# Low scores placed directly in front of the context product, and VectorE's sums and transposes interleaved, in a cross-attention block

## The chip, the cores and the metric

The kernel runs on one core of one Trainium2 chip. The metric is the device time of one execution, in microseconds. Three executions of the kernel before took 1654.61, 1655.78 and 1656.57 us, with a median of 1655.78 us. One further execution was profiled; its own time was 1652.77 us, and the span from its first to its last instruction was 1651.0 us.

## The reference

The block is one transformer layer with cross attention: 128 sequences of 128 tokens, 256 features, 16 heads of 16, a hidden layer of 1024, all in float32. Query i may see only keys j < i, so query 0 sees none and its attention is set to zero.

```python
q = (query @ Wq + bq).reshape(b, s, 16, 16).transpose(0, 2, 1, 3)
k = (key @ Wk + bk)...            # the same for k and v
scores = jnp.einsum('bhqd,bhkd->bhqk', q, k) / jnp.sqrt(16)
scores = jnp.where(j < i, scores, -1e30)
attn = jax.nn.softmax(scores, axis=-1);  attn = attn.at[:, :, 0, :].set(0.0)
ctx = jnp.einsum('bhqk,bhkd->bhqd', attn, v)
x = layer_norm(query + ctx @ Wo + bo, ln1_g, ln1_b)
out = layer_norm(x + jax.nn.relu(x @ W1 + b1) @ W2 + b2, ln2_g, ln2_b)
```

## The kernel before

Two sequences make a pair, and there are 64 pairs. The loop at line 778 makes one **step** for each pair p from 2 to 63. A step is a software pipeline over several pairs: it computes the scores and the softmax of pair p, the context and the first norm of pair p-1, the projections of pair p+1, and the feed-forward layers of pairs p-2 (`hidden`) and p-3 (`second`). The order on TensorE (PE), VectorE (DVE), ScalarE (ACT) and GpSimd (POOL) is exactly the order of the calls in the loop, because a manual schedule is set for these four engines. Only SyncE (SP), which issues most of the transfers, is put in order by the scheduler.

The queries of a sequence are split in two halves of 64. The upper half (`hi` = 1) can see all 128 keys, the lower half (`hi` = 0) only the first 64, so the lower half has half the work. `scores(p, hi)` is a set of small matmuls, with weights of 32 rows by 64 columns. `mask` adds the mask on DVE out of PSUM, `maximum` finds the row maximum on DVE and subtracts it on POOL, `exponential` runs on ACT, and `sums` adds up the rows and takes reciprocals on DVE and multiplies on POOL. These parts work on 8 of 16 heads at a time for the upper half (`ONE`, `TWO`) and on all 16 for the lower half (`ALL`).

The weights of the softmax have to be transposed for the context product. `turn(p)` does this in two stages: three transposes of 32x32 blocks on DVE write the tile `tb`, and then 16 transfers issued by SP move the blocks across the partitions into the tile `pT` (line 409). `weigh(p)` is the context product, made of small matmuls with weights of 128 rows by 32 columns that read `pT`: for every m and s first the lower half (`vd`, line 443), then the upper half (`vz`, line 451). `context` copies its result on ACT, and `attention_out` multiplies by Wo. `attention_sum` adds the residual on DVE and takes the mean and variance (`stats`); POOL makes the deviation out of them (lines 490 and 491), and `norm1` applies it.

`hidden` and `second` are the two feed-forward products, with weights of 128x128. `feed(...)` takes them in half units: 16 matmul records each in the trace. In the steady state a step has `second(p-3, 0)`, `second(p-3, 1)` and both halves of `hidden(p-2)`. `finish` multiplies by the gain and adds the bias of the second norm on POOL, and `store` issues the output transfer on ACT's queue (line 547). `values_out` issues another transfer on ACT's queue (`vd<-vz`, line 313).

The first steps have a table of their own (`plan`, line 770), because there is not yet a feed-forward product to be done. There `turn_x1_on_pe` transposes the normed tokens on PE. Later `turn_x1` does it with one DVE transpose and five transfers (lines 244 and 247).

In the built program every transfer of SP and of ACT signals its landing on one of eight semaphores, which are taken in turn in the order of the program. A transfer waits at its issue until the transfer eight places ahead of it in that order has landed, whichever of the two engines issued it, unless an earlier wait of its engine covers this already.

The order of the calls within a steady step, up to the transposes, is:

```python
scores(p, 1); feed(first); scores(p, 0)
feed(then); weigh(p - 1); context(p - 1)
queries(p + 1); attention_out(p - 1); keys(p + 1); values(p + 1)
feed(finally_)          # both halves of hidden(p - 2)
```

Of the kernel before, what the change touches and what calls it, by code (L numbers as in the profile page):

```python
# [8 lines left out]
F32 = mybir.dt.float32  # L9
# [10 lines left out]
def tile_cross_attention_block(  # L20
# [56 lines left out]

    blocks_of, tokens_of = {}, {}

    def load(ps):  # L80

        n = len(ps)
        for which, src in (("x", x), ("c", c)):
# [303 lines left out]

    def turn(p):  # L390


        st = states[p]
        tb = soft.tile([P, NS, (H + HH) * 32], F32, tag="tb", name=f"tb_{p}")
        at = 0
        for hi in (1, 0):
            sm = st["sm", hi].rearrange("p h j -> p (h j)")
            for t in range(sm.shape[1] // 1024):
                nc.vector.transpose(  # L399
                    tb[:, :, at : at + 256].rearrange("p j (n a) -> p n j a", a=32),  # L400
                    sm[:, t * 1024 : (t + 1) * 1024].rearrange(
                        "p (n j a) -> p n j a", j=NS, a=32
                    ),
                )
                at += 256
        pT = soft.tile([P, NS, (H + HH) * 32], F32, tag="pT", name=f"pT_{p}")
        for i in range(NS):
            for j in range(NS):
                nc.sync.dma_start(  # L409
                    pT[32 * j : 32 * j + 32, i, :], tb[32 * i : 32 * i + 32, j, :]  # L410
                )
        st["pT"] = pT.rearrange("p i (n a) -> p i n a", a=32)
# [19 lines left out]
    def weigh(p):  # L432

        st = states[p]
        pT = st.pop("pT")
        pc = bank(f"pc_{p}")

        for m in range(KC):
            for s in range(2):
                at = (m * 2 + s) * P  # L440
                blocks = slice(2 * s, 2 * s + 2)
                for j in range(NS):
                    nc.tensor.matmul(  # L443
                        pc[32 * j : 32 * j + 32, at : at + HP],
                        st["vd"][:, s, 4 * m + j].rearrange("p e d -> p (e d)"),
                        pT[:, blocks, H + 2 * j + m, :],
                        start=True, stop=True,
                    )
                for e in range(2):
                    for j in range(NS):  # L450
                        nc.tensor.matmul(  # L451
                            pc[32 * j : 32 * j + 32, at + HP : at + P],
                            st["vz"][:, s, 4 * m + j, 2 * e : 2 * e + 2, :].rearrange(
                                "p e d -> p (e d)"
                            ),
                            pT[:, blocks, 4 * j + 2 * m + e, :],
                            start=(e == 0), stop=(e == 1),
                        )
        st["pc"] = pc
# [33 lines left out]
    def attention_sum(p):  # L493
        st = states[p]
        t1 = st["t1"] = ffn.tile([P, 2, D], F32, tag="t1", name=f"t1_{p}")
        nc.vector.tensor_tensor(
            t1, st.pop("po").rearrange("p (s d) -> p s d", s=2), st.pop("xb"), ALU.add
        )
        stats(p, t1, 1)
        deviation(p, 1)  # L500

    def norm1(p):
# [187 lines left out]
                    done.append(p)  # L690
        return done

    alone = (2, 3)

    def both(what, p):
        return [(what, p, 0), (what, p, 1)]
# [48 lines left out]
    attention_out(0)  # L745
    exponential(1, 1, TWO)
    attention_sum(0)
    queries(2)
    sums(1, 1, ONE)
    norm1(0)  # L750
# [7 lines left out]
    for which in "xc":  # L758
# [9 lines left out]


    plan = {  # L770
        2: ([("hidden", 0, 1)], both("second", 0), both("hidden", 1)),
        3: ([("second", 1, 0)], [("second", 1, 1)], [("hidden", 2, 0)]),
        4: ([("hidden", 2, 1)], [("second", 2, 0)], [("second", 2, 1)]),
        5: ([("hidden", 3, 0)], [("hidden", 3, 1)], [("second", 3, 0)]),
        6: ([("second", 3, 1)], [("hidden", 4, 0)], [("hidden", 4, 1)]),
    }
    waiting, late = [], []
    for p in range(2, NP):
        soon, end = p + 1 < NP, p == NP - 1
        first, then, finally_ = plan.get(  # L780
            p, ([("second", p - 3, 0)], [("second", p - 3, 1)], both("hidden", p - 2))
        )
        scores(p, 1)
        mask(p, 1, 0)
        maximum(p, 1, ONE)
        feed(first)
        mask(p, 1, 1)
        maximum(p, 1, TWO)
        scores(p, 0)
        mask(p, 0, 0)  # L790
        mask(p, 0, 1)
        exponential(p, 1, ONE)
        maximum(p, 0, ALL)
        exponential(p, 1, TWO)
        feed(then)
        sums(p, 1, ONE)
        sums(p, 1, TWO)
        summed = late + sum_up(first + then)
        exponential(p, 0, ALL)
        sums(p, 0, ALL)  # L800
        for q in waiting:
            finish(q)
        weigh(p - 1)
        context(p - 1)
        if soon:
            queries(p + 1)
        attention_out(p - 1)
        if not end:
            turn(p)
        attention_sum(p - 1)  # L810
        if soon:
            keys(p + 1)
        if p + 2 < NP:
            for which in "xc":
                tokens(p + 2, which)
        norm1(p - 1)
        if p > 5:
# [6 lines left out]
        if p <= 5:  # L824
            turn_x1_on_pe(p - 1)
        residual1(p - 1)
        for q in summed:
            stats(q, states[q]["t2"], 2)
        if soon:
            add_bo(p + 1)  # L830
        if p % 2 == 0 and p + 4 < NP:
            load([p + 4, p + 5])
            load_tokens(p // 2 + 2)
        for q in summed:
            scale_and_shift(q)
        feed(finally_[:1])
        if end:
            turn_on_pe(p, 1, range(4))
        feed(finally_[1:])
        late = sum_up(finally_)  # L840
        for q in summed:
            norm2(q)
        waiting = summed
# [9 lines left out]
    attention_out(p)  # L853
    second(p - 2, 1, range(FC // 2, FC))
    attention_sum(p)
    second_sum(p - 2)
    hidden(p - 1, range(FC))
    norm1(p)
# [76 lines left out]
```

## Time and profile before

| | busy in us, share of the span | instructions |
|---|---|---|
| PE, matmuls | 1615.4 (98%) | 16524 |
| PE, weight loads | 1342.8 (81%) | 16524 |
| DVE | 1312.6 (80%) | 1983 |
| POOL | 1275.4 (77%) | 1108 |
| ACT | 766.9 (46%) | 1505 |
| span 1651.0 us; profiled execution 1652.77 us; median 1655.78 us | | |

A matmul row in the trace is the time that one matmul is in the array; matmuls overlap, so the time that a block takes is read from the start of its first matmul to the start of what comes next. From the ninth step on, the first matmul of the upper scores comes every 24.77 to 24.82 us. Steps 2 to 8 took 30.95, 25.71, 26.67, 26.67, 21.35, 25.14 and 24.94 us by the same measure. The transfers of a step that matter here, with their median time from issue to landing in the page: 16 times `pT<-tb` 2.2 us, `out_dram<-t` 3.4 us, `vd<-vz` 2.7 us, `x1t<-tbx` 1.8 us, `x1T<-x1t` 3.3 us. Loads of x and of the context bring two pairs at a time, by 4 transfers each every second step.

### The profile page before, as it was taken

How to read it: one execution, taken by the hardware profiler on the slowest of the kernel's cores; microseconds unless marked ns; L12 is line 12 of the kernel's file. 1: busy time of each engine (PE TensorE's matmuls, PEld its weight loads, DVE VectorE, ACT ScalarE, POOL GpSimd, SP SyncE). 2: the span in 40 equal slices, each digit the busy share in tenths (PEclk: the TensorE clock that was granted, in tenths of full speed). 3: DMA queues.
4: the chain of work that ended last, by engine and by line, in shares of the span. 5: the costliest groups of instructions: out<-in, count | busy, mean ns of one | idle time of the engine just before them, and what ended most of it. 6: DMA issues, size and time to landing. Idle time of an engine off the chain costs nothing.

```text
span 1651.0 us, 41181 instructions
## 1 busy us (share of the span) xinstructions
PE 1615.4 (98%) x16524; PEld 1342.8 (81%) x16524; DVE 1312.6 (80%) x1983; ACT 766.9 (46%) x1505; POOL 1275.4 (77%) x1108
## 2 busy tenths in 40 slices
PE   7998999999999999999999999999999999999997
PEld 5777888888888888888888888888888888888876
DVE  4767888888888888888888888888888888888852
ACT  4544444444444444444444444444444444444442
POOL 4766878878878878878878878878878878878873
PEclk9999999999999999999999999999999999999999
DMA  8444456566556566655666556565656575556330
GB/s 162 88 104 100 104 138 136 127 151 133 129 128 135 130 148 134 125 133 135 129 146 135 127 130 136 130 146 128 134 134 133 130 149 128 126 134 133 92 87 19
DMA packets 478973, 208.28 MB, mean 126 GB/s; under 512 B 352064, under 2 KB 447296, under 8 KB 478784
## 3 DMA queue, kind: packets, MB, share of 16 engines
q1 hardware_dynamic: 394192, 180.72, 50.3%
q10 hardware_dynamic: 84592, 24.93, 6.2%
q8 instruction: 131, 2.15, 0.6%
q14 instruction: 58, 0.48, 0.1%
HBM read 69.22 MB, written 31.98 MB: 61 GB/s over the span
## 4 chain that ended last, share of the span: by engine, by line
PE 89%; DVE 5%; POOL 3%; issue 1%; DMA 1%; ACT 1%; SPq 1%; ACTq 0%; POOLq 0%; DVEq 0%
PE py L627 25%; PE ph L611 25%; PE pq L267 7%; PE pss L333 7%; PE pk L267 6%; PE pv L299 6%; PE po L470 6%; PE pc L451 3%; PE pc L443 3%; DVE sm L350 1%; DVE nmx L361 1%; POOL sm L383 1%; POOL sm L362 1%; PE py L639 1%; SPq L409 1%
## 5 line engine op out<-in xcount | busy, mean ns | idle before, releaser
L362 POOL TENSOR_TENSOR sm<-sm,nmx 128x1024 f32<-128x1024 f32 x192 | 364.3, 1898 | 219.4 <-DVE nmx L361 219.4
L611 PE MATMUL ph<-x1T,w 128*128 128x256 f32 x2048 | 454.5, 379 | 2.5 <-ACT x1T L601 2.5
L627 PE MATMUL py<-w,hT 128*128 128x256 f32 x1952 | 453.5, 385 | 0.0
L611 PEld LDWEIGHTS ph<-x1T,w 128*128 128x128 f32 x2048 | 388.3, 190 | 57.4 <-ACT x1T L601 3.5
L627 PEld LDWEIGHTS py<-w,hT 128*128 128x128 f32 x1952 | 361.0, 190 | 76.8 <-ACT hT L617 21.9
L350 DVE TENSOR_TENSOR sm<-pss,neg 128x1024 f32<-128x1024 f32 (+1 forms) x256 | 237.9, 950 | 212.6 <-PE pss L333 199.2
L369 ACT ACTIVATE sm<-sm 128x1024 f32<-128x1024 f32 x192 | 203.0, 1057 | 354.0 <-POOL sm L362 344.6
L383 POOL TENSOR_TENSOR sm<-sm,rs 128x1024 f32<-128x1024 f32 x192 | 359.2, 1898 | 2.6 <-DVE rs L382 2.4
L617 ACT ACTIVATE hT<-ph,b1e_c 128x256 f32<-128x256 f32 x512 | 214.1, 470 | 193.5 <-PE ph L611 159.6
L399 DVE STREAM_TRANSPOSE tb<-sm 128x1024 f32<-128x1024 f32 x183 | 220.4, 1231 | 32.2 <-POOL sm L383 22.3
L361 DVE TENSOR_REDUCE nmx<-sm 128x8 f32<-128x1024 f32 (+1 forms) x192 | 234.3, 1220 | 6.6
L381 DVE TENSOR_REDUCE su<-sm 128x8 f32<-128x1024 f32 (+1 forms) x192 | 229.6, 1196 | 1.0 <-ACT sm L369 0.8
L289 ACT ACTIVATE kT<-pk,bkh,half 128x256 f32<-128x256 f32 x256 | 123.6, 563 | 161.7 <-PE pk L267 161.7
L267 PE MATMUL pq<-xT,wq 128*128 128x256 f32 x512 | 130.8, 399 | 3.2 <-ACT xT L669 3.2
L333 PE MATMUL pss<-kT,qT 32*64 32x256 f32 (+1 forms) x4096 | 126.7, 335 | 1.7 <-ACT kT L289 1.3
L470 PE MATMUL po<-wo,cxT 128*128 128x256 f32 x512 | 121.3, 379 | 1.7 <-ACT cxT L463 1.2
L516 POOL TENSOR_TENSOR x1b<-x,g_r 128x512 f32<-128x512 f32 x64 | 81.3, 1271 | 53.7 <-DVE x L508 53.7
L267 PE MATMUL pk<-cT,wk 128*128 128x256 f32 x512 | 121.1, 379 | 1.0 <-ACT cT L669 1.0
L299 PE MATMUL pv<-wv,cT 128*128 128x256 f32 x512 | 121.1, 379 | 0.0
L333 PEld LDWEIGHTS pss<-kT,qT 32*64 32x64 f32 x4096 | 76.3, 131 | 49.1 <-issue 40.6
L267 PEld LDWEIGHTS pq<-xT,wq 128*128 128x128 f32 x512 | 94.2, 194 | 20.3 <-ACT xT L669 3.6
L470 PEld LDWEIGHTS po<-wo,cxT 128*128 128x128 f32 x512 | 97.1, 190 | 15.3 <-ACT cxT L463 1.4
(82 smaller groups left out, 1765.8 us busy)
## 6 DMA issues: line engine op xcount, KB each, us to landing
pT<-tb SPq DMA_DIRECT2D x976, 96.0 KB, 2.2
out_dram<-t ACTq DMA_DIRECT2D x63, 256.0 KB, 3.4
xb<-in_x_dram SPq DMA_DIRECT2D x124, 128.0 KB, 3.8
cb<-in_ctx_dram SPq DMA_DIRECT2D x124, 128.0 KB, 4.7
x<-in_x_dram SPq DMA_DIRECT2D x31, 512.0 KB, 4.7
x1t<-tbx SPq DMA_DIRECT2D x232, 64.0 KB, 1.8
x1T<-x1t SPq DMA_DIRECT2D x58, 256.0 KB, 3.3
vd<-vz ACTq DMA_DIRECT2D x64, 128.0 KB, 2.7
```

The source lines that it names most:

```text
L267: nc.tensor.matmul(ps[:, m * TP : (m + 1) * TP], w[:, k, m * P : (m + 1) * P], src[:, k, :], start=(k == 0), stop=(k == KC - 1),)
L299: nc.tensor.matmul(pv[:, s * D : (s + 1) * D], st["cT"][:, k, s * P : (s + 1) * P], wv[:, k, :], start=(k == 0), stop=(k == KC - 1),)
L333: nc.tensor.matmul(sps[r // 2][s * HP : (s + 1) * HP, r % 2, m * 2 * n : (m + 1) * 2 * n].rearrange("p (e j) -> p e j", e=2), st["qT"][str ...
L350: nc.vector.tensor_tensor(st["sm", hi][:, part, :].rearrange("p (r n) j -> p r n j", r=2), st["sps", hi][t][:, :, : 4 * n].rearrange("p r ...
L361: nc.vector.tensor_reduce(nmx[:, part], sm[:, part, :], AX.X, ALU.max, negate=True)
L362: nc.gpsimd.tensor_tensor(sm[:, part, :], sm[:, part, :], nmx[:, part, None].to_broadcast([P, part.stop - part.start, n]), ALU.add,)
L381: nc.vector.tensor_reduce(su, sm[:, part, :], AX.X, ALU.add)
L383: nc.gpsimd.tensor_tensor(sm[:, part, :], sm[:, part, :], rs[:, :, None].to_broadcast([P, part.stop - part.start, n]), ALU.mult,)
L399: nc.vector.transpose(tb[:, :, at : at + 256].rearrange("p j (n a) -> p n j a", a=32), sm[:, t * 1024 : (t + 1) * 1024].rearrange("p (n j ...
L470: nc.tensor.matmul(po[:, s * D : (s + 1) * D], cxT[:, k, s, :], wo[:, k, :], start=(k == 0), stop=(k == KC - 1),)
L611: nc.tensor.matmul(ph[:, i * TP : (i + 1) * TP].rearrange("p (s i a) -> p s i a", s=2, a=32), w1[:, k, (f + i) * P : (f + i + 1) * P], st[ ...
L627: nc.tensor.matmul(st["py"][:, s * D : (s + 1) * D], st["hT"][:, f, s * P : (s + 1) * P], w2[:, f, :], start=(f == 0), stop=(f == FC - 1),)
```

## The change

Five things change.

- On PE the lower scores move behind the second half unit of the feed-forward product, so that they stand directly in front of `weigh`: upper scores, both half units, lower scores, `weigh`.
- Within `weigh`, for each m the lower matmuls (`vd`) of both sequences come first, and then the upper ones (`vz`) of both.
- On DVE the row sums of `ONE` and the sum behind `second` come before the lower masks. The row sums of `TWO`, the three transposes, the residual sum, the lower row sums and the statistics are interleaved. The third transpose comes behind the statistics. `turn` is split: `turn(p, hi, t)` is one transpose, `bring(p)` the 16 transfers. ACT's and POOL's order follow from this; POOL's `finish` and with it ACT's `store` stand behind the deviation of pair p-1.
- The loads of x stay in the even steps, and the loads of the context move to the odd steps.
- The table of the first steps is different: four half units in step 2, three in steps 3 to 5, the steady pattern from step 6. `turn_x1_on_pe` is used up to step 4 (before: 5), and in steps 3 and 4 it stands at the end of the step.

```diff
-    def turn(p):
-        st = states[p]
-        tb = soft.tile([P, NS, (H + HH) * 32], F32, tag="tb", name=f"tb_{p}")
...
+    def turn(p, hi, t):
+        st = states[p]
+        if "tb" not in st:
+            st["tb"] = soft.tile([P, NS, (H + HH) * 32], F32, tag="tb", name=f"tb_{p}")
+        at = (t if hi else 2) * 256
+        nc.vector.transpose(
...
+    def bring(p):
+        st = states[p]
+        tb = st.pop("tb")
         pT = soft.tile([P, NS, (H + HH) * 32], F32, tag="pT", name=f"pT_{p}")
...
     def weigh(p):
         for m in range(KC):
             for s in range(2):
                 for j in range(NS):        # vd, both s
...
+            for s in range(2):
+                at = (m * 2 + s) * P
                 for e in range(2):         # vz, both s
...
-        stats(p, t1, 1)
+
+    def attention_stats(p):
+        stats(p, states[p]["t1"], 1)
         deviation(p, 1)
...
-    alone = (2, 3)
+    alone = (1, 2)
...
-        2: ([("hidden", 0, 1)], both("second", 0), both("hidden", 1)),
-        3: ([("second", 1, 0)], [("second", 1, 1)], [("hidden", 2, 0)]),
-        4: ([("hidden", 2, 1)], [("second", 2, 0)], [("second", 2, 1)]),
-        5: ([("hidden", 3, 0)], [("hidden", 3, 1)], [("second", 3, 0)]),
-        6: ([("second", 3, 1)], [("hidden", 4, 0)], [("hidden", 4, 1)]),
+        2: ([("hidden", 0, 1)], both("second", 0), [("hidden", 1, 0)]),
+        3: ([("hidden", 1, 1)], [("second", 1, 0)], [("second", 1, 1)]),
+        4: ([("hidden", 2, 0)], [("hidden", 2, 1)], [("second", 2, 0)]),
+        5: ([("second", 2, 1)], [("hidden", 3, 0)], [("hidden", 3, 1)]),
...
         maximum(p, 1, TWO)
+        feed(then)
         scores(p, 0)
+        weigh(p - 1)
+        exponential(p, 1, ONE)
+        sums(p, 1, ONE)
+        summed = late + sum_up(first + then)
         mask(p, 0, 0)
         mask(p, 0, 1)
-        exponential(p, 1, ONE)
+        exponential(p, 1, TWO)
+        context(p - 1)
         maximum(p, 0, ALL)
-        exponential(p, 1, TWO)
-        feed(then)
-        sums(p, 1, ONE)
         sums(p, 1, TWO)
-        summed = late + sum_up(first + then)
-        exponential(p, 0, ALL)
-        sums(p, 0, ALL)
-        for q in waiting:
-            finish(q)
-        weigh(p - 1)
-        context(p - 1)
         if soon:
             queries(p + 1)
         attention_out(p - 1)
         if not end:
-            turn(p)
+            turn(p, 1, 0)
+        exponential(p, 0, ALL)
         attention_sum(p - 1)
+        sums(p, 0, ALL)
+        if not end:
+            turn(p, 1, 1)
+        attention_stats(p - 1)
+        if not end:
+            turn(p, 0, 0)
+            bring(p)
+        for q in waiting:
+            finish(q)
...
         if p % 2 == 0 and p + 4 < NP:
-            load([p + 4, p + 5])
+            load([p + 4, p + 5], "x")
             load_tokens(p // 2 + 2)
+        if p % 2 == 1 and p + 3 < NP:
+            load([p + 3, p + 4], "c")
```

More of the change, by code (lines that the diff above doesn't have):

```diff
@@ L78, in tile_cross_attention_block, with load @@
     blocks_of, tokens_of = {}, {}
-    def load(ps):
+    def load(ps, both="xc"):
         n = len(ps)
-        for which, src in (("x", x), ("c", c)):
+        for which in both:
+            src = x if which == "x" else c
             t = loads.tile(
@@ L386, in sums @@
         )
-    def turn(p):
+    def turn(p, hi, t):
         st = states[p]
-        tb = soft.tile([P, NS, (H + HH) * 32], F32, tag="tb", name=f"tb_{p}")
[L395 to L405, printed above, removed]
+        if "tb" not in st:
+            st["tb"] = soft.tile([P, NS, (H + HH) * 32], F32, tag="tb", name=f"tb_{p}")
+        at = (t if hi else 2) * 256
+        nc.vector.transpose(
+            st["tb"][:, :, at : at + 256].rearrange("p j (n a) -> p n j a", a=32),
+            st["sm", hi].rearrange("p h j -> p (h j)")[:, t * 1024 : (t + 1) * 1024].rearrange(
+                "p (n j a) -> p n j a", j=NS, a=32
+            ),
+        )
+    def bring(p):
+        st = states[p]
+        tb = st.pop("tb")
         pT = soft.tile([P, NS, (H + HH) * 32], F32, tag="pT", name=f"pT_{p}")
@@ L440, in weigh @@
                 at = (m * 2 + s) * P
-                blocks = slice(2 * s, 2 * s + 2)
                 for j in range(NS):
@@ L445, in weigh @@
                         st["vd"][:, s, 4 * m + j].rearrange("p e d -> p (e d)"),
-                        pT[:, blocks, H + 2 * j + m, :],
+                        pT[:, 2 * s : 2 * s + 2, H + 2 * j + m, :],
                         start=True, stop=True,
                     )
+            for s in range(2):
+                at = (m * 2 + s) * P
                 for e in range(2):
@@ L455, in weigh @@
                             ),
-                            pT[:, blocks, 4 * j + 2 * m + e, :],
+                            pT[:, 2 * s : 2 * s + 2, 4 * j + 2 * m + e, :],
                             start=(e == 0), stop=(e == 1),
@@ L747, in tile_cross_attention_block @@
     attention_sum(0)
+    attention_stats(0)
     queries(2)
@@ L816, in tile_cross_attention_block @@
         norm1(p - 1)
-        if p > 5:
+        if p > 4:
             turn_x1(p - 1)
@@ L823, in tile_cross_attention_block @@
             store(q)
-        if p <= 5:
+        if p == 2:
             turn_x1_on_pe(p - 1)
@@ L839, in tile_cross_attention_block @@
         feed(finally_[1:])
+        if p in (3, 4):
+            turn_x1_on_pe(p - 1)
         late = sum_up(finally_)
@@ L855, in tile_cross_attention_block @@
     attention_sum(p)
+    attention_stats(p)
     second_sum(p - 2)
```

## The prediction

> **What bounds the kernel now.** I read the busy shares first, then the chain of waits, then the steady state by stretches, then single steps of each engine. First the engine shares and the engine row of the chain on the page, and one 100 us stretch:
>
> ```profile
> PE 1615.4 (98%) x16524; PEld 1342.8 (81%) x16524; DVE 1312.6 (80%) x1983; ACT 766.9 (46%) x1505; POOL 1275.4 (77%) x1108
> ...
> PE 89%; DVE 5%; POOL 3%; issue 1%; DMA 1%; ACT 1%; SPq 1%; ACTq 0%; POOLq 0%; DVEq 0%
> ```
>
> ```profile
> 400.00:500.00 100.00, 100.00 (x1030) 83.32 (x1029) 83.26 (x126) 47.55 (x94) 80.35 (x69) 1.00 0.61 134
> ```
>
> PE is never idle in the steady state (the columns are width, then busy time of PE, weight loads, DVE, ACT, POOL), and its clock is full. A step is 24.78 us of matmuls end to end, so only a shorter matmul stream, or a new wait in it, can move the time. One step on PE, from the timeline:
>
> ```profile
> 808.84 1.12 PE L333 MATMUL pss<-kT,qT 32*64 32x256 f32 x32
> 809.89 3.72 PE L627 MATMUL py<-w,hT 128*128 128x256 f32 x16
> 813.54 0.84 PE L333 MATMUL pss<-kT,qT 32*64 32x128 f32 x32
> 814.31 3.72 PE L627 MATMUL py<-w,hT 128*128 128x256 f32 x16
> 817.97 0.32 PE L443 MATMUL pc<-pT,vd 128*32 128x64 f32 x8
> ...
> 819.60 1.99 PE L267 MATMUL pq<-xT,wq 128*128 128x256 f32 x8
> 821.43 1.89 PE L470 MATMUL po<-wo,cxT 128*128 128x256 f32 x8
> 823.16 1.89 PE L267 MATMUL pk<-cT,wk 128*128 128x256 f32 x8
> ```
>
> From start to start, `po` takes 1.73 us for 8 records, 0.216 each. The `py` block of 16 should take 3.46 and takes 3.65: between two blocks of small matmuls it pays 0.19 us for the switch into full-size weights and out of them. I count all times below from the first upper-score matmul of a step (here 808.84) and write them as t.
>
> What feeds the context product is the queue of SP and the store on ACT's queue. SP's issues and the store of an even step, then the store's landing there and in the odd step after it:
>
> ```profile
> 826.24 10.70 SPq L409 DMA_DIRECT2D pT<-tb  x16
> ```
>
> ```profile
> 828.41 0.69 ACTq L547 DMA_DIRECT2D out_dram<-t  x1
> ```
>
> ```profile
> DMA to landing us min/median/max: 3.4/3.4/3.4
> ```
>
> ```profile
> DMA to landing us min/median/max: 2.6/2.6/2.6
> ```
>
> And what SP's `pT` issues wait for, over the whole span (total, times, longest):
>
> ```profile
> SPq L409 <- DVE tb L399: 332.2, 61, 19.7
> SPq L409 <- DMA vd<-vz: 80.5, 29, 4.4
> ```
>
> The second line is an odd one: nothing in `pT` depends on `vd`. It is the shared completion semaphore: in odd steps the third `pT` issue stands eight places behind that transfer of ACT. It costs some 2.8 us there, and is harmless: the run issued from 900.57 has its last issue at 913.4 and lands 2.2 later, at 915.6, and `weigh` begins at 917.06. The smallest such slack in the steady steps is about 1.1 us.
>
> **The change part by part.**
>
> *Lower scores moved.* The two `py` blocks become one of 32 records: 32 x 0.216 + 0.19 = 7.10 us in place of 3.65 + 3.66. The lower scores now lead straight into `weigh`, small into small: the cost of entering `weigh` stays. Gain 0.2 us a step, and a step of PE is then 24.57: upper scores to t 1.05, `py` to 8.15, lower scores to 8.92, `weigh` to 10.55, `pq` 12.38, `po` 14.11, `pk` and `pv` 17.57, `ph` 24.57.
>
> *Order within `weigh`.* Before, its first `vz` run takes 0.36 us from start to start and the later ones 0.22: PE is taking the semaphore waits for the second eight of the 16 transfers, and loses 0.14 us. Now these waits come behind 8 records in place of 24, so less work covers them: between -0.14 (the lower scores cover them) and +0.25 (all four waits, 0.11 us each by the trace, exposed). I take 0, the row as it is.
>
> *DVE's order.* Its work is unchanged, 20.65 of 24.78 us. The upper masks and maxima run at t 1.2 to 6.0 as before. The `ONE` sums wait for ACT until 6.8, the lower masks for PE until 9.05; both gaps come out of DVE's 4.1 idle us. The first transpose ends at 14.0. The residual sum then waits for `po`, whose last record ends at 14.3. Behind it, by rows of the trace: residual sum 0.69, lower sums 1.64, second transpose 1.19, statistics 1.09, third transpose 1.25. So the 16 transfers can be issued at t 20.2; before it was 826.24 - 808.84 = 17.4. That is 2.8 us later, with 0.4 us less of a step to cover it.
>
> *POOL and ACT.* The statistics end at 18.97; the deviation takes 1.1 (to 20.1), then `finish` 2.63 (824.86 to 827.49), so the store is issued at t 22.75, where it was 828.41 - 808.84 = 19.57. Queued behind it on ACT are the relu copies: the first ends at 24.3, and the `second` that needs it, and its PSUM bank, comes at 25.6, so this is covered by 1.3 us. On POOL the residual, `add_bo` and second-norm work behind `finish` end at 28.2, and the next subtraction is due at 28.3: covered, by 0.1 us only; DVE's own wait there gives some 0.8 more.
>
> *SP's queue.* In the new program order the store stands eight places ahead of the eighth `pT` transfer in even steps, and of the seventh in odd ones (before: the fifteenth, and the fifth; it was landed in time). This is the wait that the change adds. Unhindered, these issues would come at t 24.6 and 24.0. Behind the waiting one are 8 or 9 issues of 0.635 us, and behind those `weigh`.
>
> How long the store takes decides. **The Trainium skill** (DMA: Bandwidth & Descriptors, Anatomy of one DMA) gives about 2.0 us fixed plus bytes over 436 GB/s, most of it the receipt from memory: for 256 KB an estimate of 2.6. The trace shows 2.43 to 3.14 us in 12 of 13 odd steps, where SP stands still at that moment (the rule), and 3.32 to 5.18 us with a median of 3.64 in the 14 even steps with a recorded landing, where `pT` transfers are in flight beside it. After the change they are in flight in every step, so I take the row, 3.64: landed at t 26.4. Then the last `pT` is issued 8 x 0.635 or 9 x 0.635 later and lands 2.2 us after: t 33.6 in even steps, 34.25 in odd ones. `weigh` of the next step is due at 24.57 + 8.92 = 33.5. By the rule it would be 32.55 and 33.2, and no wait.
>
> By the row PE waits 0.1 and 0.75 us. About half of the 16-issue runs before also hold one more gap of 0.6 to 1.2 us; half of it falls behind the store, 0.2 on average. The last transfer is needed only 0.1 us into `weigh`. Mean wait 0.55. It is not paid back: `po`, the statistics, `finish` and the store all hang on `weigh`, so each delay is handed to the next step, and one of 24.57 cannot catch up. A step becomes 25.1, +0.35 against 24.78, on the 55 steps from 9 to 63: **+19 us**.
>
> *Loads split.* 4 of the 8 loads (0.64 us and more each) change the step. They lie on SP between `x1T` and the next `pT`, some 5 us of slack; nothing.
>
> *First steps.* Steps 2 to 6 took 131.35 us. With the new table step 2 has one half unit less (-3.5), but its norm is later: behind the third transpose, at about t 26 against 22.2, so PE waits some 4.8 us in front of the transposes, and runs cold after. Steps 3 to 5 have no such long wait (the transposes stand behind `second`), about 23, 23.6 and 21.8 us; step 6 gets the bill, as its `pT` is late by some 3.3 us. TensorE: Matmul & The Clock Gate (Part 1) lets the clock fall after an idle window of about 3.4 us; this trace shows 0.70 and 0.79 of full speed after a wait of only 2.88 us (134 to 141 us), 1.5 us lost. By the rule step 6 takes 26.3, by the row 27.9; I take the row. Sum 128.8: -2.5, range -7 to +5. *Tail:* the last step's POOL wait of 1.6 us in front of its transposes goes: -1.5.
>
> **Sum.** 1652.77 (the profiled execution, span and what lies around it) + 19 - 2.5 - 1.5 = 1667.8. The median of the runs shown is 3.0 above the profiled execution, so **1671 us**.
>
> **Rivals.** *The store is not in the way* (the other side of mine is faster): it lands within 2.9 us in odd steps and 3.5 in even ones, and PE stays the bound at 24.57: 55 x -0.21 - 4 = -15.5, **1640**. For it: the odd-step landings and the rule. Against it: what sets the even-step landings is in flight beside it from now on. *The gain is eaten in `weigh`* (+0.25): 24.82 a step, +2 - 4, **1654**. For it: four waits with 8 records to cover them. Against: PE takes such waits ahead, under the lower scores. *POOL's 0.1 us is used up as well*, or the extra gaps all fall behind the store: a step of 25.6, +45 - 4, **1697**. That the change does not do what it says is excluded: the built order shows it.
>
> **How the numbers follow.** Mine 0.51 (1658 to 1690), store harmless 0.26, gain eaten in `weigh` 0.11, the larger loss 0.12. The range 1640 to 1695 takes in both ends of the store. Within 0.2% is about what a measurement of this kernel can tell from no change. Faster 0.28, same 0.08, slower 0.64.
>
> **What would show it.** Steps of about 25.1 us, odd ones longer than even ones; PE waiting in `weigh` for `pT`; SP's seventh or eighth `pT` issue waiting for `out_dram`; the store at t 22.7 and landing over 3 us later. I am wrong if steps are 24.6 and the store lands in 2.6, or if PE waits elsewhere (the scores, or the bank of `py`).

## The result and the profile after

The changed kernel takes **1649.12 us** (median of 5 runs, 1646.46 to 1651.47) against 1655.56 us of the kernel before in the same comparison: a ratio of 0.9959, with a 95% interval of 0.9946 to 0.9973. It is 0.4% faster. The forecast was 1671 us, slower than before; the direction was wrong, though the time lies in the range.

The profiled execution of after has a span of 1647.7 us (before 1651.0). From the page, the busy shares of the engines and the engine row of the chain that ended last:

```profile
PE 1597.6 (97%) x16520; PEld 1340.7 (81%) x16520; DVE 1376.1 (84%) x1984; ACT 754.1 (46%) x1503; POOL 1287.3 (78%) x1108
...
PE 58%; DVE 14%; SPq 9%; DMA 9%; POOL 6%; issue 2%; ACT 1%; DVEq 0%; ACTq 0%; POOLq 0%
```

PE has 18 us less work (1597.6 against 1615.4), but the span has fallen by 3 only. The chain, which was PE for 89%, now leaves PE for 42% of the span. The same 100 us stretch that was full of PE work before shows where:

```profile
400.00:500.00 100.00, 98.55 (x1029) 82.87 (x1028) 87.30 (x126) 46.66 (x93) 80.97 (x69) 1.00 0.58 132
```

PE now waits 1.45 us in these four steps. Between 280 and 1550 us it waits nowhere but in front of the context product (total, times, longest):

```profile
PE pc L444 <- DMA x1t<-tbx: 3.7, 7, 1.1
PE pc L444 <- DMA pT<-tb: 1.8, 3, 1.0
```

The product reads no `x1t`; such a transfer signals on the same semaphores as the `pT` ones. In before the same list is empty. One step on PE, from the timeline of after (start, length, then the group):

```profile
805.10 1.12 PE L334 MATMUL pss<-kT,qT 32*64 32x256 f32 x32
806.15 7.17 PE L632 MATMUL py<-w,hT 128*128 128x256 f32 x32
813.26 0.69 PE L334 MATMUL pss<-kT,qT 32*64 32x128 f32 x32
813.88 0.67 PE L444 MATMUL pc<-pT,vd 128*32 128x64 f32 x16
814.34 0.66 PE L454 MATMUL pc<-pT,vz 128*32 128x64 f32 x32
814.79 0.43 PE L444 MATMUL pc<-pT,vd 128*32 128x64 f32 x16
815.01 0.66 PE L454 MATMUL pc<-pT,vz 128*32 128x64 f32 x32
815.60 1.99 PE L268 MATMUL pq<-xT,wq 128*128 128x256 f32 x8
```

Read from start to start: the one `py` block takes 7.10 us (median of the steady steps), where the two blocks took 3.65 each; the lower scores take 0.62, where they took 0.77 when a `py` block came behind them; and the context product takes 1.72 in this step (1.75 by the medians of its parts over the steady steps), where it took 1.65. An undisturbed step is 24.51 us. The chain through one step of after shows what lies behind the waits of PE (start, length, what). This step is itself an undisturbed one; in others the same chain ends later.

```profile
826.05 1.36 POOL t L549
827.41 0.02 issue
827.43 2.60 DMA out_dram<-t
830.03 0.02 issue
830.04 0.51 SPq L411
```

This is the wait that the prediction named: GpSimd's `finish`, then the store on ACT's queue, then SP's eighth `pT` issue, which may go on only when the store has landed. The list of SP's waits has it as well (total, times, longest):

```profile
SPq L411 <- DMA out_dram<-t: 53.2, 52, 2.3
```

But the store lands early. Its time from issue to landing between 400 and 800 us, in before and then in after:

```profile
DMA to landing us min/median/max: 2.4/3.6/5.2
```

```profile
DMA to landing us min/median/max: 2.4/2.5/4.1
```

The whole difference can be laid out over the span, from the starts of the upper scores in both traces:

| | before, us | after, us | difference | forecast |
|---|---|---|---|---|
| start to step 0 | 17.22 | 17.34 | +0.1 | 0 |
| steps 0 to 8 | 221.62 | 221.19 | -0.4 | -2.5 (steps 2 to 6) |
| steps 9 to 62, mean | 24.783 | 24.626 | -0.157, 54 times: -8.5 | +0.35, 55 times: +19 |
| from step 63 to the end | 73.85 | 79.31 | **+5.5** | -1.5 |
| span | 1651.0 | 1647.7 | -3.3 | |

So the questions are three: why did the store land in 2.5 us and not in 3.6, what is the rest of the forecast's chain worth, and what happened in the last step?

### The profile page after: what moved, and what is told of

It reads as the page before. It is cut to its first block, busy times and chain, and to the rows that moved or that the text cites. A ratio compares the mean times of both kernels' runs of the same rounds, so it can differ in the third digit from the quotient of the medians.

```text
span 1647.7 us, 41234 instructions
## 1 busy us (share of the span) xinstructions
PE 1597.6 (97%) x16520; PEld 1340.7 (81%) x16520; DVE 1376.1 (84%) x1984; ACT 754.1 (46%) x1503; POOL 1287.3 (78%) x1108
## 4 chain that ended last, share of the span: by engine, by line
PE 58%; DVE 14%; SPq 9%; DMA 9%; POOL 6%; issue 2%; ACT 1%; DVEq 0%; ACTq 0%; POOLq 0%
PE ph L616 17%; PE py L632 13%; SPq L411 8%; PE pq L268 6%; PE po L473 5%; PE pk L268 4%; PE pv L300 4%; DMA out_dram<-t 4%; PE pss L334 4%; DVE tb L397 3%; DVE su L382 3%; DMA x1t<-tbx 3%; PE pc L454 2%; POOL t L549 2%; POOL t L548 2%
## 5 line engine op out<-in xcount | busy, mean ns | idle before, releaser
L384 POOL TENSOR_TENSOR sm<-sm,rs 128x1024 f32<-128x1024 f32 x192 | 364.8, 1900 | 111.7 <-DVE rs L383 110.6
L632 PE MATMUL py<-w,hT 128*128 128x256 f32 x1952 | 438.2, 382 | 0.3 <-ACT hT L622 0.3
L632 PEld LDWEIGHTS py<-w,hT 128*128 128x128 f32 x1952 | 365.8, 190 | 70.4 <-ACT hT L622 22.6
L622 ACT ACTIVATE hT<-ph,b1e_c 128x256 f32<-128x256 f32 x512 | 196.0, 488 | 236.5 <-POOL t L549 191.8
L397 DVE STREAM_TRANSPOSE tb<-sm 128x1024 f32<-128x1024 f32 x183 | 224.3, 1225 | 12.7 <-issue 4.8
L542 ACT ACTIVATE t<-t,nb,sd 128x256 f32<-128x256 f32 x126 | 68.8, 593 | 124.9 <-POOL nb L534 124.9
L334 PE MATMUL pss<-kT,qT 32*64 32x256 f32 (+1 forms) x4096 | 117.1, 335 | 1.5 <-ACT kT L290 1.3
L268 PEld LDWEIGHTS pk<-cT,wk 128*128 128x128 f32 x512 | 97.3, 190 | 14.4 <-ACT cT L674 1.2
```

The lines of the kernel that those rows point to most:

```text
L268: nc.tensor.matmul(ps[:, m * TP : (m + 1) * TP], w[:, k, m * P : (m + 1) * P], src[:, k, :], start=(k == 0), stop=(k == KC - 1),)
L384: nc.gpsimd.tensor_tensor(sm[:, part, :], sm[:, part, :], rs[:, :, None].to_broadcast([P, part.stop - part.start, n]), ALU.mult,)
L397: nc.vector.transpose(st["tb"][:, :, at : at + 256].rearrange("p j (n a) -> p n j a", a=32), st["sm", hi].rearrange("p h j -> p (h j)")[:, ...
L622: nc.scalar.activation(st["hT"][:, f + i, :], ph[:, i * TP : (i + 1) * TP], AF.Relu, bias=b1e_c[:, f + i : f + i + 1], scale=1.0,)
L632: nc.tensor.matmul(st["py"][:, s * D : (s + 1) * D], st["hT"][:, f, s * P : (s + 1) * P], w2[:, f, :], start=(f == 0), stop=(f == FC - 1),)
```

## The experiments

"Mean step" is the mean of steps 9 to 62, and "tail" the time from the start of step 63 to the end of the span, both from the profiled execution. Ratios are to the kernel before, run beside each.

| run | median us | ratio, 95% interval | mean step | tail |
|---|---|---|---|---|
| after | 1649.12 | 0.9959 [0.9946, 0.9973] | 24.626 | 79.3 |
| e1_pe_alone | 1837.23 | 1.1119 [1.1088, 1.1151] | 27.70 | 77.1 |
| e2_pe_act | 1763.09 | 1.0661 [1.0643, 1.0679] | 26.27 | 78.2 |
| e1_weigh_before | 1643.44 | 0.9935 [0.9921, 0.9950] | 24.540 | 78.5 |
| e2_late | 1661.42 | 1.0042 [1.0026, 1.0058] | 24.800 | 80.0 |
| e3_later | 1679.47 | 1.0154 [1.0137, 1.0171] | 25.115 | 79.9 |
| e2_early | 1638.95 | 0.9905 [0.9891, 0.9920] | 24.525 | 71.9 |
| e1_tail | 1643.74 | 0.9933 [0.9917, 0.9950] | 24.615 | 75.8 |
| e2_plan_before | 1670.62 | 1.0092 [1.0071, 1.0114] | 24.636 | 79.0 |
| e3_best | 1632.76 | 0.9874 [0.9859, 0.9888] | 24.456 | 71.9 |
| e4_first | 1629.93 | 0.9856 [0.9839, 0.9872] | 24.456 | 72.0 |
| e1_vd_behind, e3_vd_ahead | 1654.52, 1709.01 (one run each) | | 24.78, 25.68 | 73.9, 78.2 |

### Why the store lands early

In the kernel before, the transfer `vd<-vz` stands on ACT's queue 0.7 to 1.0 us ahead of the store. In after the store comes 3.8 us behind it, since it waits for `finish`. The first run swaps the two in the kernel **before**.

```diff
 def values_out(p):
...
-        nc.scalar.dma_start(st["vd"][HP:], st["vz"][:HP, :, :, 2:4, :])
...
         for q in waiting:
             store(q)
+        if soon:
+            move_values(p + 1)      # the vd<-vz transfer
```

> The kernel before with one edit: the vd<-vz transfer is issued behind the store on ACT's queue and not in front of it. Asked is why the store landed in 3.3 to 5.2 us in the even steps of before, and in 2.55 us in after. Theory A (the vd transfer 0.8 us ahead of it on the same queue is what slows it): the store lands in about 2.6 us in even steps too. Theory B (the pT transfers that SP goes on issuing while the store is in flight slow it; in after SP stands still then, waiting for the store itself): even steps stay at 3.3 us or more. The time itself should stay within 0.3% of before.

The store's landing between 400 and 800 us in this run:

```profile
DMA to landing us min/median/max: 2.4/2.6/3.0
```

The median falls from 3.6 to 2.6 us and the longest from 5.2 to 3.0. Only 8 of the 16 landings of this stretch are recorded in before and 6 in this run. Over steps 9 to 62, in the even steps, 14 recorded landings of before took 3.3 to 5.2 us, and 10 of this run 2.6 to 3.1. They are short although SP issues `pT` transfers 0.6, 1.2, 2.3 and 3.0 us behind the store in the even steps (before: 0.3, 0.9, 2.1 and 2.8). The counter-test makes the reverse edit in **after**, with SP standing still as in after:

```diff
         for q in waiting:
...                                   # the tile spare
+            nc.scalar.copy(spare, states[q]["t2"][:, :, :4])   # waits for finish
+        if soon:
+            move_values(p + 1)
+        for q in waiting:
             store(q)
```

> The changed kernel with the vd<-vz transfer moved on ACT's queue directly ahead of the store (a small copy out of t makes it wait for finish first), pT transfers being in flight beside both, and SP standing at the store's landing as in after. Asked is what makes a landing slow. Theory A (vd directly ahead on the same queue): the store, issued about 0.7 us behind vd, lands in 3.3 us or more, as in the even steps of before. Theory B (SP's further issues, which the wait for the store stops here): it lands in 2.5 to 2.7 us, as in after.

```profile
DMA to landing us min/median/max: 3.4/3.8/4.6
```

Every recorded landing in this stretch (11 of 15) is 3.4 us or more; over steps 9 to 62 the shortest of 36 is 3.2. Both runs agree with theory A: `vd<-vz` directly ahead of the store, with `pT` transfers in flight beside both, makes the landing slow. `pT` alone does not in most steps; a few landings of after are long without it (up to 4.1 us), and no run shows why. The time of 1709 us is not to be read as the price of this, as SP's issues now also wait for `vd` itself (119 us in the list of SP's waits). One part stays open: in the odd steps of before, where SP stood still on both sides, `vd` was just as near and most landings were short, so both neighbours seem to be needed; no run separates them, and none puts `vd<-vz` ahead of the store on another queue.

### Whether the rest of the forecast's chain holds

Added copies on ACT in front of the store make it as late as the forecast had it. They add work and change no value.

```diff
         for q in waiting:
+            for i in range(2):          # 3 in the second run
...                                   # the tile spare
+                nc.scalar.copy(spare, states[q]["t2"])
             store(q)
```

> The changed kernel with two added copies on ACT (128x512 into a spare tile, 0.58 us each) in front of the store, in the steady steps: the store is issued at t 23.5 in place of 22.3 and lands at about 26.1, where the prediction had it (26.4). Asked is whether the rest of the prediction's chain holds when the landing is as late as it said. Theory 1 (it does: the eighth or seventh pT issue waits for the landing, the last lands at t 33.3 to 34, and the delay is handed from step to step): steps of 24.9 to 25.1 us on the mean, 1665 to 1675. Theory 2 (the slack takes it up, or the delay is not handed on): mean step below 24.75, below 1657.

> As the run with two added copies in front of the store, with three: the store is issued at t 23.65 and lands at t 26.2, within 0.2 us of the 26.4 that the prediction took. With the store issued 0.67 us later than in after (two copies) the mean step went from 24.63 to 24.80. Theory 1 (the chain of the prediction was right and only the landing mis-sized): now nearly every later microsecond counts, steps of 25.0 to 25.2 us on the mean, 54 x 0.4 = 22 us over after and more: 1670 to 1680. Theory 2 (the delay is taken up by the slack of single steps): below 24.9, 1662 to 1665.

With two copies the store is issued 0.67 us later than in after, less than I expected: in one step the two copies run from 831.62 to 832.89, and the issue starts at 832.28. The mean step is 24.800, between the two theories, and the kernel is **slower than before** (1.0042). With three copies the store is issued at t 23.6 or later; its landing takes 2.5 us on the median, so it lands at t 26.0 to 26.2 in steps without another delay, near the 26.4 of the forecast. The mean step is 25.115 us, where the forecast had 25.1. The close match is in part luck: in two steps of 28.1 and 28.2 us the clock fell behind the waits (0.94 on the mean of the step), and without these two the mean is 25.00. SP's waits for the store rise from 53.2 to 82.4 and 111.8 us, and PE still waits in front of the context product alone. So the chain was right from the landing on, to about 0.1 us a step. The wait falls in the step behind an odd one, as the forecast's working has it: without those two, even steps take 25.11 us and odd ones 24.89. Its list of signs had the two the wrong way round.

The other direction takes the store off the chain: `finish` is split, its product in POOL's gap in front of the lower subtraction, its sum in front of the lower multiplication, and the store is issued behind the `kT` copies.

```diff
         summed = late + sum_up(first + then)
+        for q in waiting:
+            gain(q)                 # finish, first half
...
         sums(p, 1, TWO)
+        for q in waiting:
+            shift(q)                # finish, second half
...
-        for q in waiting:
-            finish(q)
         if soon:
             keys(p + 1)
+        for q in waiting:
+            store(q)
...
-        for q in waiting:
-            store(q)
```

> The changed kernel with finish split in two: its product fills POOL's gap of 1.26 us in front of the lower subtraction, its sum the gap of 1.2 us in front of the lower multiplication, and ACT issues the store behind the kT copies, at about t 17.9 in place of 22.3. Theory 1 (the only thing that still lengthens single steps is SP's eighth or seventh pT issue waiting for the store's landing; without it the last pT is issued 1.3 to 2 us earlier, and the extra gaps of SP no longer reach the context product): all steady steps 24.51 to 24.54 us (mean now 24.63), and ACT no longer stands at the store in the last step, so that the tail falls from 79.3 to 74 us: 11 us off, 1638. Theory 2 (another transfer gives the wait, vd<-vz eight places ahead, or POOL's two added operations push the softmax back by more than they save): mean step 24.6 or more, 1644 or more.

Theory 1 holds: the store is issued at t 16.6 (earlier than the 17.9 I had given), no wait of SP for it is left in the list, nearly all steps are 24.50 to 24.54 us, and their mean is 24.525. The 0.10 us a step between this and after is all that the wait still cost: 54 x 0.10 = 5.5 us. The tail falls to 71.9.

### What PE's order needs from the other engines

> The kernel before with one edit: the lower scores stand behind the second half unit, directly in front of the context product; VectorE's, ScalarE's and GpSimd's orders, the loads and the first steps stay. From the trace of after, the PE part alone is worth 7.302-7.104 = 0.20 us (one block of 32 records for two of 16) and 0.77-0.62 = 0.15 us (small matmuls lead into small ones) a step, 0.35 together. Theory 1 (the other parts carry the gain, VectorE's order above all): DVE now idles from t 6 to t 9 in front of the lower masks, the row sums of the upper half follow at 11.5, the first pT transfer is issued at t 20.4 or later and lands after t 33.4, so that PE waits in the context product: steps of 24.9 us or more, 1660 or more. Theory 2 (PE's order alone is the gain): steps of 24.4 to 24.5 us, 1640.

```diff
         maximum(p, 1, TWO)
+        feed(then)
         scores(p, 0)
...
         exponential(p, 1, TWO)
-        feed(then)
```

The PE move alone makes the kernel 11% slower, and by neither theory's way. PE does not wait for `pT` in any steady step; it waits in front of `po` (PE's waits: total, times, longest):

```profile
PE po L470 <- ACT cxT L463: 164.5, 62, 4.5
```

On ACT, the copy `cxT` stands behind the lower exponential, which follows the lower scores, and these now start 3.5 us later (t 8.15 against 4.70). The wait is 2.6 us in every steady step. In 42 of the 54 the step takes 27.34 us; in the other 12 the clock falls to 0.94 on the mean, and the step takes 28.9 or 29.0. The next run keeps the PE move and takes that copy ahead of the lower exponential.

```diff
         exponential(p, 1, TWO)
...
+        weigh(p - 1)
+        context(p - 1)          # the copy cxT on ACT
         exponential(p, 0, ALL)
...
-        weigh(p - 1)
-        context(p - 1)
```

> The kernel before with the PE move and one more edit: the context product and ACT's copy of its result (cxT) come in front of the lower exponential. With the PE move alone PE waited 2.8 us in every step for that copy, which stood on ACT behind the lower exponential. Theory 1 (ACT's place of the copy was all that the PE move needed; what is left is the vd gate at the fourth pT issue of odd steps, which lands pT at t 34.7 there, 1.5 us late): even steps 24.4 us, the step behind an odd one 25.5 to 26, mean 25.1 to 25.3, 1670 to 1685. Theory 2 (VectorE's old order alone is too late for the context product in both kinds of steps): steps of 25.5 us or more throughout, 1690 or more.

```profile
PE ph L611 <- DVE t L496: 60.2, 54, 1.6
```

The wait for `cxT` is gone, steps are 26.30 us, and PE waits again, 1.5 and 0.7 us in turn, now in `ph`: its PSUM bank is freed by the residual sum on DVE, which reads `po` and stands behind all three transposes. (In every second step it waits for the sum behind `second` as well, in `pk`.) Theory 2 had DVE's order as the cause, though through a bank and not through `pT`. So PE's order needs the others. The place of one copy on ACT is worth 1.04 us a step (27.34 to 26.30). From there to the 24.51 of after it is 1.79 us; the rows put this wait down to DVE's sums, but after differs in more than DVE's order, and no run moves that order alone. Both are more than the 0.35 us that PE's order saves on PE itself.

### The order inside the context product

```diff
         for m in range(KC):
             for s in range(2):
                 for j in range(NS):        # vd
...
-            for s in range(2):
-                at = (m * 2 + s) * P
                 for e in range(2):         # vz
```

> The changed kernel with the old order inside the context product (per m and s: 8 vd, then 16 vz). In the trace of after this product takes 1.746 us from its start to pq's start, before 1.647. Theory 1 (the waits for the last transfers stand behind 8 records in place of 24 and are exposed): the product falls back to 1.65 and the undisturbed step from 24.51 to 24.41 us, 5 us over the whole. Theory 2 (the order inside is free, the 0.10 us comes from standing right behind the lower scores): product 1.75, step 24.51, no change.

With the old order (8 `vd`, 16 `vz` for each m and s) the undisturbed step is 24.44 us and the mean 24.540, 0.086 less than after. Theory 1 had 24.41. So the new order costs 0.07 us. The rows of after show where: from start to start the first `vd` run takes 0.46 us (813.88 to 814.34) and the second, of the same size, 0.22. In the old order the first `vz` run is the slow one, with 0.38 us (0.36 in before) against 0.22 for a later one: 0.24 lost against 0.16. That this loss is the waits for the second half of the transfers, which come behind 8 records and not behind 24, fits the rows but is not shown by itself.

### The last step

In after, PE's timeline shows this in the last step of the loop, and ACT's the reason:

```profile
1581.72 3.72 PE L616 MATMUL ph<-x1T,w 128*128 128x256 f32 x16
1585.27 1.04 PE L427 MATMUL ptp<-ident,sm 128*128 128x128 f32 x8
1591.58 1.94 PE L427 MATMUL ptp<-ident,sm 128*128 128x128 f32 x8 [5.27 <-issue]
1593.31 5.24 PE L616 MATMUL ph<-x1T,w 128*128 128x256 f32 x16
```

```profile
1590.21 0.38 ACTq L552 DMA_DIRECT2D out_dram<-t  x1
1590.64 1.57 ACT L622 ACTIVATE hT<-ph,b1e_c 128x256 f32<-128x256 f32 x4 [7.71 <-POOL t L549]
```

The profile names no releaser for this wait (`<-issue`). I read it so: the transposes need PSUM banks that the relu copies free. The copies stand on ACT behind the store, and ACT holds there until POOL's `finish`, which the change put behind the deviation. In a steady step the three projections of pair p+1 give ACT the time; the last step has none. PE's clock falls behind the wait: the granted clock is 0.50 from 1591 to 1595 us, and the same `ph` block of 16 takes 5.24 us, where the one ahead of the wait takes 3.72.

```diff
-        for q in waiting:
-            finish(q)
+        if not end:
+            for q in waiting:
+                finish(q)
...                                   # store the same
+        if end:                      # behind the relu copies
+            for q in waiting:
+                finish(q)
+                store(q)
```

> The changed kernel with one edit: in the last step of the loop alone, finish and store of pair 60 come behind the relu copies of the hidden layer, on POOL and ACT. In after, PE waits 5.27 us there in front of the transposes and its clock falls to 0.66 in the next 10 us; from the start of the last step to the end it takes 79.3 us against 73.9 before. Theory 1 (ACT stands at the store until POOL's finish is done, the relu copies stand behind it and hold the PSUM banks that the transposes need): the wait goes, the tail falls to about 73 us, 6 us off the whole. Theory 2 (the transposes wait for the softmax, which POOL finishes at 18.1 us of the step): the wait stays over 3 us, no change over 1 us.

The edit moves the store of pair 59 (the expectation says 60). The wait of 5.27 us is gone, as theory 1 has it, and the tail is 75.8 us, 3.5 us less, where I expected 6: the store now holds up the copies of the lower transposes, and PE waits 2.2 us for them in front of the last context product. In `e2_early`, where `finish` is done long before, neither wait is left (71.9).

### The first steps

```diff
-    alone = (1, 2)
+    alone = (2, 3)
...                                   # plan of before, steps 2 to 6
-        if p in (3, 4):
-            turn_x1_on_pe(p - 1)
```

> The changed kernel with the table of the first steps of before, and the transposes of the normed tokens on PE where they stood. Asked is what the new table brings. The prediction gave it 2.5 us for steps 2 to 6. Theory 1: without it the steps 0 to 8 take 2 to 5 us more than the 221.2 of after. Theory 2 (in after step 5 is short of a half unit, 22.7 us, VectorE's work does not fit into it, its pT comes late and step 6 pays 5 us for it): the old table is no slower, 216 to 221 us.

The old table under the new orders makes steps 0 to 8 take 241.3 us, against 221.2 of after. This is far outside both theories. The largest of PE's waits is for the norm, in front of the transposes on PE:

```profile
PE ptn L234 <- DVE x L513: 19.3, 7, 5.9
```

In after the same wait is 6.8 us in all; the rest of the 20 us was not followed. With the old orders the same table took 221.6. So the new orders of the engines need the new table: without it they would cost 20 us here, and more than the whole gain. This figure is of one execution; the four of this run differ by 7 us.

### Together

`e3_best` has the edits of `e2_early` and `e1_weigh_before`, and `e4_first` a further table.

> Two of the edits together: finish split into POOL's two gaps with the store behind the kT copies (mean step 24.525 and tail 71.9 by itself, 1638.95 us), and the old order inside the context product (undisturbed step 24.44 in place of 24.51 by itself). Theory 1 (the two are independent, both on PE's path): steps of 24.44 to 24.47, 54 x 0.07 = 4 us less than the first alone: 1635. Theory 2 (with the store gone from the path the order inside matters no more): 1639.

```diff
-        2: ([("hidden", 0, 1)], both("second", 0), [("hidden", 1, 0)]),
-        3: ([("hidden", 1, 1)], [("second", 1, 0)], [("second", 1, 1)]),
-        4: ([("hidden", 2, 0)], [("hidden", 2, 1)], [("second", 2, 0)]),
-        5: ([("second", 2, 1)], [("hidden", 3, 0)], [("hidden", 3, 1)]),
+        2: ([("hidden", 0, 1)], both("second", 0), []),
+        3: ([("hidden", 1, 0)], [("hidden", 1, 1)], [("second", 1, 0)]),
+        4: ([("second", 1, 1)], [("hidden", 2, 0)], [("hidden", 2, 1)]),
+        5: (*([i] for i in both("second", 2)), both("hidden", 3)),
```

> The best version so far with another table of the first steps: three half units in steps 2, 3 and 4, four in step 5 (so far 4, 3, 3, 3), the same work in sum. In after, steps 2 and 6 take 31.6 and 29.7 us; step 5, short of a half unit, takes 22.7, and its pT lands 38.3 us after its start while the context product is due at 31.5. Theory 1 (step 6 is long because step 5 is shorter than VectorE's work needs, and step 2 because it has more PE work ahead of a wait for the norm): step 2 falls by the 3.5 us of its half unit to about 28, step 5 takes 24.5, step 6 24.5 to 26: 6 to 9 us off, 1625. Theory 2 (VectorE's work alone sets the sum of these steps, wherever the half unit stands): steps 2 to 6 stay within 2 us of 131.5, 1632.

The two edits add: `e3_best` takes 1632.76 us, 2 us less than expected. The other table takes steps 2 to 6 from 131.5 to 129.0 us: steps 2 and 6 fall by 6.2 and 6.6, but 3, 4 and 5 rise by 5.5, 0.3 and 4.5. That is nearly theory 2: moving a half unit moves the wait. A further us comes from steps 0 and 1 (39.8 against 40.8), which the run with the tail edit also shows without this table, so no edit is its cause. At **1629.93 us** it is the fastest of all, but its interval overlaps that of `e3_best`: what the table gives is read from the traces, and the times alone do not prove it.

## Why the prediction was wrong, step by step

- **PE's bound and the two blocks made one**: right. 7.104 us measured, 7.10 forecast.
- **Lower scores and context product**: small misses that nearly cancel. The lower scores lose their switch to full-size weights too (0.77 to 0.62; the forecast kept 0.77), and the context product takes 0.10 longer, 0.07 of it by the order inside, where 0 was taken in a range of -0.14 to +0.25. The undisturbed step is 24.51, forecast 24.57.
- **DVE's order, the store's issue, the gate on SP**: right in place and nearly in time. First `pT` issue t 19.76 (forecast 20.2), store t 22.33 (22.75), the waiting issue the eighth in even steps and the seventh in odd ones. DVE's work, which the forecast took as unchanged, grew by 1.0 us a step (last section), and its slack took this up. The slack of 1.1 us that the forecast gave the `pT` runs of before was misread: in step 45 the last transfer lands 0.55 us ahead of `weigh`, and in step 27 one lands as `weigh` begins. Nothing rests on it.
- **The store's landing: this step failed.** The prediction wrote "After the change they are in flight in every step, so I take the row, 3.64" (they: the `pT` transfers), and set it against an estimate of 2.6 us. The Trainium skill (DMA: Bandwidth & Descriptors, Anatomy of one DMA) gives the figures of that estimate for transfers issued by GpSimd; this store is issued by ACT, so its agreement with the trace was not a given. Measured: 2.55 in most steps, with the `pT` transfers in flight. The row was a true measurement but came with a neighbour that the change took away: `vd<-vz` directly ahead on the same queue. The shift of 2.8 us, charged as a cost, also moved the store out of its reach. In sum the steady steps miss the forecast by 27.5 us (+19 to -8.5). Not all of it is the landing's length, as the store was also issued 0.4 us earlier than forecast. An estimate from the mean steps of after, e2_late and e3_later by their landings (24.9, 25.45, 26.1): a store issued at 22.75 and landing 2.55 us later would give about 24.75 us a step. So some 19 us go to the length and some 7 to the issue.
- **The slack of ACT (1.3 us)**: right for the steady steps, and not followed into the last one. There the forecast saw POOL's wait of 1.6 us go and wrote -1.5; measured +5.5, by ACT's place of the store, which the same paragraph had named.
- **First steps**: 131.4 us for steps 2 to 6, forecast 128.8, before 131.35. Step 6 is the main miss, 29.7 against 27.9 (steps 4 and 5 add 0.8 and 0.9, step 2 takes 0.9 less); its `pT` was late, as said, and the clock fell behind the wait. From the stretches of that step (width, PE busy, then the clock):

```profile
168.00:172.00 4.00, 1.38 (x43) 1.00 0.50 121
172.00:174.00 2.00, 1.52 (x83) 0.80 0.46 113
174.00:176.00 2.00, 2.00 (x20) 0.50 0.66 123
176.00:178.00 2.00, 2.00 (x9) 0.84 0.87 173
```

  The wait was 3.10 us, and the clock fell to 0.50. The Trainium skill (TensorE: Matmul & The Clock Gate, Part 1) gives an idle window of about 3.4 us; the forecast followed the trace here, rightly, and still took too little. In e1_pe_alone waits of 2.6 us were at times enough.
- **Rivals**: "the store is not in the way" came nearest by its mechanism (the landing within 2.9 us), but its 1640 had neither the tail nor the single late steps in it. By number 1654 ("the gain is eaten in `weigh`") is nearest, by luck: `weigh` lost 0.10 us a step and not 0.25, and the tail's 7 us, which no rival had, stand in the measured time.

## What to carry to other kernels

A transfer's duration taken from a trace belongs to what stands beside and ahead of it in that trace; when a change moves the transfer, ask which of these neighbours move along before the row is used. Where the sign of a change hangs on one landing, find the margin: here 0.67 us at the store's issue were enough to turn 0.4% faster into 0.4% slower. And an instruction that waits at the head of an in-order engine has to be followed into the first and last steps too, where the work that covers it is missing.

## What the runs showed of the hardware beyond that

DVE's norm of `x` (two instructions a step) has the same shapes everywhere, but not the same duration. The group between 400 and 1500 us (count, busy us, mean ns, idle before) in before, then after, then `e2_early`:

```profile
L508 DVE TENSOR_SCALAR x<-t,mv,sd 128x256 f32<-128x256 f32 x90 | 33.1, 411 | 0.0
```

```profile
L513 DVE TENSOR_SCALAR x<-t,mv,sd 128x256 f32<-128x256 f32 x90 | 74.3, 868 | 0.0
```

```profile
L513 DVE TENSOR_SCALAR x<-t,mv,sd 128x256 f32<-128x256 f32 x90 | 31.3, 392 | 0.0
```

In after each of these 90 runs beside POOL's `finish`, in the other two kernels none; with `finish` moved away it is back at 392 ns. This explains most of the 64 us of DVE's time that after shows above before. The Trainium skill (Trainium Architecture — The Big Picture, What this means for kernel authors) says that DVE and GpSimd contend for a shared port pair by an exclusive lock; the rows of `x` agree with that, and no run tests the port by itself. It does not hold every DVE instruction: in after the transpose `xT<-xb` runs beside the same `finish` in all 45 steps and takes 670 ns, as in `e2_early` (669), where it does not. Here DVE had the slack.

SP's further gaps of 0.9 to 2.4 us between `pT` issues, at places that differ from step to step, are in all kernels and stay unexplained. They and the few long landings, together with the gate, go with the late steps of after; without the gate (`e2_early`) the slack takes them up.
